# Value products of 512 columns with channels on the partitions, turned by VectorE and sixteen transfers, in a cross-attention kernel; set-up reordered

## The chip, the cores and the metric

The kernel runs on one core of a Trainium2 chip. The core has five engines that work side by side: TensorE (PE, with its weight loads shown apart as PEld), VectorE (DVE), ScalarE (ACT), GpSimd (POOL) and SyncE (SP), which here only issues transfers. SP and ACT issue transfers on hardware queues, POOL on a software queue; all are carried by the core's 16 DMA engines. The metric is the device time of one execution in microseconds (us); lower is better. The kernel before takes 1952.8 us, the median of three runs (1952.07 to 1952.91).

## The reference

The arrays `x` and `y` are (32, 256, 1024) in fp32: 32 batches of C = 256 channels and N = 1024 positions. The weights `w_qk`, `w_v`, `w_t` are 256 x 256.

```
x_q = einsum('oc,bcn->bno', w_qk, y)
x_k = einsum('oc,bcn->bon', w_qk, x)
x_v = einsum('oc,bcn->bon', w_v, x) + b_v
energy    = einsum('bnc,bcm->bnm', x_q, x_k)
attention = softmax(energy, axis=-1)
attention = attention / (1e-07 + attention.sum(axis=1, keepdims=True))
x_r = einsum('bcn,bnm->bcm', x_v, attention)
x_r = relu(einsum('oc,bcn->bon', w_t, x - x_r) + b_t)
return x + x_r
```

## The kernel before

**Weights are folded.** Set-up multiplies weights among themselves once: `gw` is w_qk with itself, so that the energy is y (gw x) and no query product is left; `vw` is w_v with w_t, so that what attention gathers is already through w_t; `tw` is w_t transposed. Biases are folded likewise (`xbias`, `ubias`, `nbias`).

**Three forms.** Every operand of a large product is kept in three forms, HIGH, LOW and REST (`FORMS = 3`), in fp32r: a rounded high part and two corrections with a scale of `UP = 4096` between them. A product of two operands is the sum over the three pairs of forms, all in one accumulation. With the 256 channels in two blocks of 128 (`KC = 2`), an output of 128 rows and 512 columns takes 3 x 2 = 6 matmuls, and one of 128 x 1024 takes 12. Such a set of twelve is the unit that the text calls a group.

**A batch** consists of these groups on TensorE, each named by a token:

- `k0`, `k1`: keys of the next batch, one block of 128 channels each (`keys`, `channels`); ScalarE and two passes of VectorE make the three forms `gf`.
- `v0`, `V1`: values, one half of the positions each (`values`). In the kernel before, x is the stationary operand: a matmul takes 128 positions as weights and `vw` as the 256 moving columns, so a half takes 4 x 3 x 2 = 24 matmuls of 256 columns and comes out with positions on the partitions, as attention needs it. `right` makes the three forms `uf[q]`: one pass of ScalarE and two of VectorE, straight from PSUM.
- `W0`, `W1`: the straight product of x with `tw` (`straight`), put by ScalarE into `xe`.
- `E0` to `E7`: energy for 128 query positions by 1024 keys (`energy`), then the softmax: a minimum over the row by VectorE, exponential with row sum on ScalarE, reciprocal, and the three forms `ef` by ScalarE, VectorE and GpSimd. VectorE adds the column sums up in `acc`.
- `A0` to `A7`: attention (`attention`), which adds `uf` times `ef` into banks 4 to 7 over the eight steps; the forms are taken in the order HIGH, REST, LOW (`ORDER`).
- `S` sums the columns (VectorE), `O` finishes the batch (`finish`): VectorE divides, GpSimd adds `xe`, ScalarE takes the ReLU, GpSimd adds x, SP stores. `X` loads the next x, `Y2` and `Y3` the next halves of y; GpSimd's queue makes two of the corrections by transfers that add.

**PSUM** has eight banks, used as four pairs. Pairs 2 and 3 hold the attention sums from A0 to the division; before A0 they are lent to the groups whose token ends in `^`. All others alternate between pairs 0 and 1. `uf` has one buffer for each half, `ef` four, `yf` two.

**What sets the order.** `Plan` takes each operation with an engine, a planned duration, a planned lag and the names that it reads and writes. TensorE works in the order of the tokens in `FIRST`, `STEADY`, `BEFORE` and `LAST` (first, middle, last but one and last batch) and `SET_UP`. On the other engines, transfers included, the planner runs through time and takes the operation that is due first; the order that comes out is fixed for each engine, and an engine does not go past an instruction that waits. The names and durations exist for the planner only: at run time an instruction waits for what the tiles that it really touches require. All calls go through one helper, so nearly every line of the profile reads L187, and the tile names tell the operations apart.

Lines touched: the token strings (124 to 138), `load_y` (276), `values` (368), `energy` (393), `finish` and its kin (485 to 586), the set-up's loads (602 to 612), `square`, `weights`, `turned`, `value_weights`, `biases` (626 to 747).

Of the kernel before, what the change touches and what calls it, by code (L numbers as in the profile page):

```python
# [16 lines left out]
class Plan:  # L17
# [124 lines left out]
def kernel(  # L142
# [28 lines left out]
    NE = 4  # L171

# [61 lines left out]

    few = const.tile([P, P], F32, name="few")
# [13 lines left out]
    xo = one.tile([P, N], F32, name="xo")  # L249
    xe = one.tile([P, KC, N], F32, name="xe")  # L250
# [8 lines left out]
    def pair(j):  # L259
        return banks[:, 2 * j : 2 * j + 2]  # L260
# [15 lines left out]
    def load_y(q, direct=False):  # L276
# [5 lines left out]
        by_sync(7.0, [], ["yr"], lambda: sync.dma_start(r, from_))  # L282
# [85 lines left out]
    def values(b, q, j_pair):  # L368
        p = pair(j_pair)
        for t in range(HT):  # L370
            for j in ORDER:

                def of(t=t, j=j):
                    for k in range(KC):
                        matmul(
                            p[:, t // 2, ts(t % 2, C)], xf[:, j, k, ts(q * HT + t, P)], vw[:, j, k],
                            t % 2 == 0 and j == ORDER[0] and k == 0, j == ORDER[-1] and k == KC - 1,
                        )

                on_pe(  # L380
                    KC, C, [f"vw{j}{k}" for k in range(KC)] + [f"xf{j}{k}{q}" for k in range(KC)], [in_pair(j_pair)[t // 2]], of
                )
        right(j_pair, [uf[q][:, j] for j in range(FORMS)], [[f"uf{q}{j}"] for j in range(FORMS)])
# [9 lines left out]
    def energy(b, n, jp):  # L393
        s, e = (b * MH + n // HT) % NY, n % NE
        both, at, f = pair(jp), in_pair(jp), ef[n % NE]
        for h in range(MH):
            for j in ORDER:

                def of(h=h, j=j):
                    for k in range(KC):  # L400
                        matmul(
                            both[:, h], yf[s][:, j, k, ts(n % HT, P)], gf[:, j, k, ts(h, MB)],
                            j == ORDER[0] and k == 0, j == ORDER[-1] and k == KC - 1,
                        )

                on_pe(KC, MB, [f"yf{s}{j}"] + [f"gf{j}{k}" for k in range(KC)], [at[h]], of)
# [51 lines left out]
    def sums(b):  # L458
# [11 lines left out]
        def small_ops():  # L470
# [9 lines left out]
            1.25, ["sc"], ["rc"],  # L480
# [3 lines left out]
    def finish(b):  # L484
        for c in range(KC):

            def of(c=c):
                p = flat(pair(2 + c))
                on_dve(
                    N, in_pair(2 + c) + ["rc", "bias"], [f"z{c}"],  # L490
# [7 lines left out]
                by_sync(6.0, [], ["xo"], lambda: sync.dma_start(xo, x[b, ts(c, P)]))  # L498
# [17 lines left out]
    def divided(c):  # L516

        for h in range(MH):

            def of(c=c, h=h):  # L520
                p = pair(2 + c)[:, h]
                on_dve(
                    MB, [in_pair(2 + c)[h], "rc", "bias"], [in_pair(2 + c)[h]],
                    lambda: dve.scalar_tensor_tensor(p, p, ubias[:, c], rc[:, ts(h, MB)], ALU.add, ALU.mult),
                )

            of()

    def beside(b, c):

        for h in range(MH):

            def of(h=h):
# [4 lines left out]
                    MB, [in_pair(2 + c)[h], "rc", "bias", f"stored{c}"], [piece],  # L538
# [63 lines left out]
    for k, (by, dma) in enumerate(((by_sync, sync), (by_act, act))):  # L602
        by(2.9, [], [f"wqk{k}"], lambda k=k, dma=dma: dma.dma_start(wqk[:, k], w_qk[ts(k, P)]), early=50.0)
    for h in range(MH):
        for k, (by, dma) in enumerate(((by_sync, sync), (by_act, act))):
            by(
                3.9 + h, [], [f"xr{k}{h}"],
# [3 lines left out]
    by_sync(6.0, [], ["wt"], lambda: sync.dma_start(wt, w_t.rearrange("(k p) c -> p k c", p=P)), early=25.0)  # L611
    by_act(6.0, [], ["wv"], lambda: act.dma_start(wv, w_v.rearrange("(k p) c -> p k c", p=P)), early=25.0)
# [13 lines left out]
    def square(bank, left, right, reads, writes):  # L626
        for i in range(KC):

            def of(i=i):
                for k in range(KC):  # L630
                    matmul(
                        banks[:, bank + i, :C], left[:, k, ts(i, P)], right[:, k], k == 0, k == KC - 1
# [4 lines left out]
    def weights(to, name, bank, by, d, d_name):  # L637

        for i in range(KC):

            def of(i=i):
# [9 lines left out]
                dve_in_sbuf(  # L651
                    C // 2, [f"{d_name}{i}", "xe0"], names[LOW],
                    lambda: dve.tensor_scalar(low, dd, UP, None, ALU.mult),
                )
# [51 lines left out]
    def turned():  # L706
# [21 lines left out]
    def value_weights():  # L728
        square(
            6, wv, wtT.rearrange("p (k c) -> p k c", k=KC), ["wv", "z0", "wtT", "acc0", "acc1"],  # L730
            [f"vwin{i}" for i in range(KC)],
        )
        weights(vw, "vw", 6, -UP, work[:, KC * C : 2 * KC * C], "vwd")

    def biases():
        by_sync(7.0, [], ["bv"], lambda: sync.dma_start(bv, b_v.rearrange("(o c) -> o c", o=1).to_broadcast([P, C])))
        by_sync(7.0, [], ["bt"], lambda: sync.dma_start(bt, b_t.rearrange("(k p o) -> p k o", p=P, o=1)))
# [11 lines left out]
    def set_up(token):  # L749
# [3 lines left out]
        elif token == "T":  # L753
            turned()
# [94 lines left out]
```

## Time and profile before

| | before |
|---|---|
| median of 3 runs | 1952.8 us |
| profiled execution | 1952.31 us |
| its span, first to last instruction | 1950.5 us |
| matmuls, busy (the same count of weight loads) | 9252, 1939.1 us |
| matmuls of the values, 128 x 256 | 1536, 196.5 us |
| VectorE, ScalarE, GpSimd busy | 1553.9, 1433.5, 1253.9 us |
| granted TensorE clock, mean | 0.998 |
| first matmul of V0 in the first batch | at 18.98 us |

The span leaves out 1.8 us of the profiled execution that lie around it. Busy time of TensorE is modelled for overlapping matmuls, so the pace is better read from the starts of consecutive groups. A row of instructions gives the total busy time, the mean of one, and after the bar how long the engine stood idle just before them and what ended that. A wait says who waited for whom, for how long in all, how often, and the longest.

### The profile page before, as it was taken

The page shows a single profiled execution, that of the slowest core. Times are in us where ns is not written, and L with a number is a line of the kernel's source. Part 1 is how long each engine was busy: PE and PEld are TensorE (multiplying, and loading weights), DVE is VectorE, ACT ScalarE, POOL GpSimd, SP SyncE. Part 2 cuts the span into 40 slices and gives each one's busy share as a digit, 9 for nine tenths or more (in the row PEclk, how much of TensorE's full clock was granted, in tenths as well). Part 3 has the DMA queues.
Part 4 walks back from the last instruction along what each step waited for, and adds up shares of the span by engine and source line. Part 5 has one row for each costly group of instructions (what it writes and reads, how often), then busy time and mean ns, then how long its engine had stood idle before and what let it go on. Part 6 is the DMA issues. An engine that isn't in the chain of part 4 may idle for free.

```text
span 1950.5 us, 25236 instructions
## 1 busy us (share of the span) xinstructions
PE 1939.1 (99%) x9252; PEld 1634.3 (84%) x9252; DVE 1553.9 (80%) x2177; ACT 1433.5 (73%) x1859; POOL 1253.9 (64%) x645
## 2 busy tenths in 40 slices
PE   8999999999999999999999999999999999999998
PEld 7888888888888888888888888888888888888887
DVE  7787887877887778878788877887877887778887
ACT  5778776787767877667877678776787767777675
POOL 4667665766656666566766577665766656666564
PEclk9999999999999999999999999999999999999999
DMA  4555545565455554455544555545564455554440
GB/s 128 129 119 141 123 108 115 119 148 123 112 105 130 140 127 118 109 125 127 137 119 104 126 119 141 125 110 111 121 149 121 116 104 128 139 130 118 110 98 33
DMA packets 81994, 234.28 MB, mean 120 GB/s; under 512 B 7504, under 2 KB 8656, under 8 KB 81872
## 3 DMA queue, kind: packets, MB, share of 16 engines
q0 software_dynamic: 35136, 98.58, 29.4%
q1 hardware_dynamic: 46032, 133.19, 21.1%
q8 instruction: 73, 1.20, 0.3%
q10 hardware_dynamic: 704, 0.92, 0.1%
q14 instruction: 49, 0.40, 0.1%
HBM read 133.56 MB, written 33.55 MB: 86 GB/s over the span
## 4 chain that ended last, share of the span: by engine, by line
PE 97%; DVE 2%; issue 0%; ACT 0%; DMA 0%; DVEq 0%
PE banks L187 97%; DVE xf L187 0%; DVE gf L187 0%; DVE ef L187 0%; DVE acc L187 0%; DVE z L187 0%; DVE vw L187 0%; DMA z<-in_L_xattn_w_qk_dram 0%; DVE small L187 0%; DVE parts L187 0%; DVE rc L187 0%; DVE xe L187 0%; DVE sc L187 0%; DVE gw L187 0%; ACT yf L187 0%
## 5 line engine op out<-in xcount | busy, mean ns | idle before, releaser
L187 POOL TENSOR_TENSOR ef<-ef 128x1024 fp32r<-128x1024 f32 x256 | 614.2, 2405 | 444.7 <-ACT ef L187 226.1
L187 PE MATMUL banks<-gf,yf 128*128 128x512 f32 x3072 | 728.4, 389 | 0.3 <-DVE gf L187 0.3
L187 PE MATMUL banks<-ef,uf 128*128 128x512 f32 x3072 | 722.5, 389 | 1.1 <-DVE acc L187 1.1
L187 PEld LDWEIGHTS banks<-ef,uf 128*128 128x128 f32 x3072 | 576.7, 188 | 121.4 <-DVE acc L187 1.1
L187 PEld LDWEIGHTS banks<-gf,yf 128*128 128x128 f32 x3072 | 574.5, 188 | 118.9 <-DVE gf L187 0.7
L187 DVE SCALAR_TENSOR_TENSOR ef<-banks,small,ef 128x512 fp32r<-128x512 f32 x512 | 378.7, 745 | 151.3 <-ACT ef L187 151.0
L187 DVE TENSOR_REDUCE small<-banks 128x1 f32<-128x1024 f32 x256 | 312.6, 1221 | 108.4 <-PE banks L187 106.3
L187 ACT ACTIVATE banks<-banks,small 128x1024 f32<-128x1024 f32 x256 | 276.9, 1082 | 134.4 <-DVE small L187 133.7
L187 ACT ACTIVATE ef<-banks,small 128x512 fp32r<-128x512 f32 x512 | 320.9, 690 | 40.5 <-DVE small L187 40.5
L187 DVE SCALAR_TENSOR_TENSOR acc<-banks,small,acc 128x512 f32<-128x512 f32 x448 | 329.7, 742 | 0.0
L187 POOL TENSOR_TENSOR z<-z,xe 128x1024 f32<-128x1024 f32 (+1 forms) x64 | 151.1, 2380 | 205.3 <-DVE z L187 205.3
L187 ACT ACTIVATE ef<-ef 128x1024 fp32r<-128x1024 f32 x256 | 268.9, 1068 | 12.5
L187 ACT ACTIVATE gf<-banks 128x1024 fp32r<-128x1024 f32 x64 | 65.3, 1021 | 190.2 <-PE banks L187 190.2
L187 PEld LDWEIGHTS banks<-vw,xf 128*128 128x128 f32 x1536 | 194.8, 194 | 8.1 <-ACT gf L187 3.3
L187 PE MATMUL banks<-vw,xf 128*128 128x256 f32 x1536 | 196.5, 285 | 2.9 <-DVE vw L187 2.9
L187 PE MATMUL banks<-xf,tw 128*128 128x512 f32 (+1 forms) x774 | 186.1, 389 | 0.8 <-DVE z L187 0.6
L187 PE MATMUL banks<-xf,gw 128*128 128x512 f32 x768 | 185.4, 390 | 0.3
L187 PEld LDWEIGHTS banks<-xf,gw 128*128 128x128 f32 x768 | 143.9, 188 | 30.9 <-DVE xf L187 0.6
L187 PEld LDWEIGHTS banks<-xf,tw 128*128 128x128 f32 x774 | 143.0, 189 | 29.5 <-DVE z L187 0.8
L187 POOL TENSOR_TENSOR z<-z,xo 128x1024 f32<-128x1024 f32 x62 | 157.7, 2544 | 9.0 <-DMA xo<-in_x_dram 9.0
L187 POOL TENSOR_TENSOR xf<-xr,xf 128x1024 fp32r<-128x1024 f32 (+1 forms) x64 | 151.2, 2388 | 5.7 <-DVE xf L187 4.6
L187 DVE RECIPROCAL small<-small 128x1 f32<-128x1 f32 x256 | 41.3, 161 | 114.8 <-ACT banks L187 113.5
(66 smaller groups left out, 1408.5 us busy)
## 6 DMA issues: line engine op xcount, KB each, us to landing
yr<-in_ctx_dram SPq DMA_DIRECT2D x64, 512.0 KB, 3.8
yf<-in_ctx_dram POOLq DMA_DIRECT2D x63, 512.0 KB, 6.7
yf<-yf POOLq DMA_DIRECT2D x63, 512.0 KB, 4.6
xo<-in_x_dram SPq DMA_DIRECT2D x62, 512.0 KB, 4.3
xr<-in_x_dram SPq DMA_DIRECT2D x62, 512.0 KB, 3.4
xf<-xf POOLq DMA_DIRECT2D x62, 512.0 KB, 6.9
out_dram<-z SPq DMA_DIRECT2D x62, 512.0 KB, 4.8
out_dram<-z SPq DMA_DIRECT2D x3, 256.0 KB, 2.1
```

What stands on the lines that cost most here:

```text
L187: self.last = getattr(self.engine, name)(*args, **kwargs)
```

## The change

**Values.** `values` now takes `vw` as the stationary operand and 512 positions as the moving columns: 12 matmuls of 512 columns, channels on the partitions. Attention still needs positions there, so the result is turned. VectorE transposes it from PSUM in blocks of 32 x 32 into a new tile `turned` (128 x 1024). Sixteen transfers on SP's queue, four for each of the four groups of 32 target partitions, put the blocks in their places in the buffer of `uf`'s REST form: each takes 32 partitions to 32 others, four runs of 64 numbers in each. The order of the columns of `vw` is permuted in `value_weights` so that the blocks fall right, and its scale is -1 in place of -4096. The forms then come from this fp32 copy in SBUF: ScalarE copies HIGH, GpSimd subtracts, ScalarE scales LOW, GpSimd subtracts again for REST. VectorE's two passes from PSUM go.

**Order.** The token strings are new. In the middle batches V1 stands first, E6 and E7 are neighbours, and `v0` moves from the end to behind A5. E0 takes its matmuls by form (HIGH, LOW, REST), both halves of the columns for each, and the others as before.

**Set-up.** The keys' matmuls of the first batch come in another order. The scaling that makes LOW of a weight goes from VectorE to ScalarE (`weights`). The LOW form of the first y is made by an adding transfer on GpSimd's queue, no longer by a subtraction on GpSimd (`Y_ON_POOL` is False). Planned durations of some loads are changed, and the loads of the first y, of the biases and of `xo` name more that the planner is to wait for.

The diff, cut to its core:

```diff
 SET_UP = (
-    "x1 x0 G fH00 T b fH10 fL10 fR00 fH11 fR11 Q fR10 fH01 fL00 y fL11 fL01 fR01"
+    "x0 G fR10 x1 fH11 T fH10 fH01 fH00 Q fL00 fL10 fL11 b y fR00 fR11 fL01 fR01"
 )
 FIRST = (
-    "V0^ W1 E0 E1^ V1 E2 W0^ E3 A0 A1 E4 E5 A2 A3 E6 A4 E7 X A5 A6 k1 Y2 S A7 Y3 k0 O v0"
+    "V0^ W1^ W0^ E0^ E1 E2 V1^ E3 A0 A1 E4 E5 A2 A3 E6 E7 A4 X A5 v0 Y2 k1 A6 A7 k0 Y3 S O"
 )
 STEADY = (
-    "W1^ E0^ E1 V1^ E2 W0^ E3 Y2 A0 A1 E4 E5 A2 A3 E6 X A4 E7 Y3 A5 S k1 A6 A7 k0 O v0"
+    "V1 E0^ E1 W0^ E2 W1^ E3 A0 A1 E4 E5 X A2 A3 E6 E7 A4 S A5 v0 Y2 A6 k1 k0 A7 O Y3"
 )
 BEFORE = (
-    "E0^ E1 W1^ E2 V1^ W0^ E3 A0 A1 E4 E5 A2 A3 X E6 E7 A4 S A5 A6 k1 A7 Y2 Y3 k0 O v0"
+    "W1 E0^ E1 V1^ E2 W0^ E3 A0 X A1 E4 A2 E5 Y2 E6 A3 A4 v0 E7 k0 Y3 A5 S A6 k1 A7 O"
 )
 LAST = (
-    "V1^ E0 E1^ E2 E3 A0 A1 E4 E5 A2 A3 R E6 E7 A4 A5 A6 W0 a0 S G0 a1 D1 F1"
+    "E0 E1^ E2 R V1^ E3 A0 A1 E4 E5 A2 A3 E6 E7 A4 A5 A6 W0 a0 S G0 a1 D1 F1"
 )
...
-        by_sync(7.0, [], ["yr"], lambda: sync.dma_start(r, from_))
+        by_sync(7.0 if b else 3.5, ["xr01", "xr11"] if b == 0 else [], ["yr"], lambda: sync.dma_start(r, from_))
...
-        if direct:
+        if direct and q == 0 and Y_ON_POOL:
             on_pool(
                 N, [name[LOW], name[REST]], [name[LOW]],
...
     def values(b, q, j_pair):
-        p = pair(j_pair)
-        for t in range(HT):
+
+        both, at, u = pair(j_pair), in_pair(j_pair), uf[q]
+        for i in range(KC):
             for j in ORDER:
 
-                def of(t=t, j=j):
+                def of(i=i, j=j):
                     for k in range(KC):
                         matmul(
-                            p[:, t // 2, ts(t % 2, C)], xf[:, j, k, ts(q * HT + t, P)], vw[:, j, k],
-                            t % 2 == 0 and j == ORDER[0] and k == 0, j == ORDER[-1] and k == KC - 1,
+                            both[:, i], vw[:, j, k, ts(i, P)], xf[:, j, k, ts(q, MB)],
+                            j == ORDER[0] and k == 0, j == ORDER[-1] and k == KC - 1,
                         )
...
-        right(j_pair, [uf[q][:, j] for j in range(FORMS)], [[f"uf{q}{j}"] for j in range(FORMS)])
+                on_pe(KC, MB, [f"vw{j}{k}" for k in range(KC)] + [f"xf{j}{k}{q}" for k in range(KC)], [at[i]], of)
+        on_dve(
+            N, at, ["turned"],
+            lambda: dve.transpose(
+                turned.rearrange("p (q i r) -> p i q r", i=KC, r=G32),
+                both.rearrange("p i (q r) -> p i q r", r=G32),
+            ),
+        )
+        raw = value(u[:, REST])
+        names = [f"uf{q}{j}" for j in range(FORMS)]
+        moves = [f"{names[REST]}{a}" for a in range(NG)]
+        for a in range(NG):
+
+            def of(a=a):
+                for g in range(NG):
+                    sync.dma_start(
+                        raw[ts(a, G32)].rearrange("p (t g r) -> p t g r", t=HT, g=NG)[:, :, g],
+                        turned[ts(g, G32)].rearrange("p (t a r) -> p t a r", t=HT, a=NG)[:, :, a],
+                    )
+
+            plan.add("sync", 1.6, 6.0, ["turned"], [moves[a]], of)
+        on_act(N, moves, [names[HIGH]], lambda: act.copy(u[:, HIGH], raw))
+        on_pool(
+            N, moves + [names[HIGH]], [names[LOW]],
+            lambda: pool.tensor_tensor(u[:, LOW], raw, value(u[:, HIGH]), ALU.subtract),
+        )
+        on_act(N, [names[LOW]], [names[LOW]], lambda: act.mul(u[:, LOW], value(u[:, LOW]), UP))
+        on_pool(
+            N, [names[LOW]], [names[REST]] + moves,
+            lambda: pool.tensor_tensor(u[:, REST], raw, value(u[:, LOW]), ALU.subtract),
+        )
...
-        for h in range(MH):
-            for j in ORDER:
...
+        steps = [(j, h) for h in range(MH) for j in ORDER]
+        if n == 0:
+            steps = [(j, h) for j in (HIGH, LOW, REST) for h in range(MH)]
...
-                by_sync(6.0, [], ["xo"], lambda: sync.dma_start(xo, x[b, ts(c, P)]))
+                by_sync(6.0, ["bias"], ["xo"], lambda: sync.dma_start(xo, x[b, ts(c, P)]))
...
-                dve_in_sbuf(
-                    C // 2, [f"{d_name}{i}", "xe0"], names[LOW],
-                    lambda: dve.tensor_scalar(low, dd, UP, None, ALU.mult),
-                )
+                on_act(C, [f"{d_name}{i}", "xe0"], names[LOW], lambda: act.mul(low, dd, UP))
...
-            [f"vwin{i}" for i in range(KC)],
-        )
-        weights(vw, "vw", 6, -UP, work[:, KC * C : 2 * KC * C], "vwd")
+            [f"vwin{i}" for i in range(KC)], lambda w: w.rearrange("p (q i r) -> p i q r", i=KC, r=G32),
+        )
+        weights(vw, "vw", 6, -1.0, work[:, KC * C : 2 * KC * C], "vwd")
```

More of the change, by code (lines that the diff above doesn't have):

```diff
@@ L171 @@
     NE = 4
+    Y_ON_POOL = False
     const = ctx.enter_context(tc.tile_pool(name="const", bufs=1))
@@ L249 @@
     xo = one.tile([P, N], F32, name="xo")
+    turned = one.tile([P, N], F32, name="turned")
     xe = one.tile([P, KC, N], F32, name="xe")
@@ L395, in energy, with of @@
         both, at, f = pair(jp), in_pair(jp), ef[n % NE]
-        for h in range(MH):
-            for j in ORDER:
[L399 to L403, printed above, removed]
-                        )
-                on_pe(KC, MB, [f"yf{s}{j}"] + [f"gf{j}{k}" for k in range(KC)], [at[h]], of)
+        steps = [(j, h) for h in range(MH) for j in ORDER]
+        if n == 0:
+            steps = [(j, h) for j in (HIGH, LOW, REST) for h in range(MH)]
+        begun = {h: [j for j, g in steps if g == h] for h in range(MH)}
+        for j, h in steps:
+            def of(j=j, h=h):
+                for k in range(KC):
+                    matmul(
+                        both[:, h], yf[s][:, j, k, ts(n % HT, P)], gf[:, j, k, ts(h, MB)],
+                        j == begun[h][0] and k == 0, j == begun[h][-1] and k == KC - 1,
+                    )
+            on_pe(KC, MB, [f"yf{s}{j}"] + [f"gf{j}{k}" for k in range(KC)], [at[h]], of)
         p = flat(both)
@@ L624, with square @@
     )
-    def square(bank, left, right, reads, writes):
+    def square(bank, left, right, reads, writes, blocks=lambda w: w):
         for i in range(KC):
@@ L631, in of @@
                     matmul(
-                        banks[:, bank + i, :C], left[:, k, ts(i, P)], right[:, k], k == 0, k == KC - 1
+                        banks[:, bank + i, :C], left[:, k, ts(i, P)], blocks(right[:, k]), k == 0, k == KC - 1
                     )
```

28 lines of the change are left out of this document (13 added, 15 removed).

## The prediction

> **What bounds the kernel now.** First the page: the span, the busy times, and the chain of work that ended last.
>
> ```profile
> span 1950.5 us, 25236 instructions
> PE 1939.1 (99%) x9252; PEld 1634.3 (84%) x9252; DVE 1553.9 (80%) x2177; ACT 1433.5 (73%) x1859; POOL 1253.9 (64%) x645
> ...
> PE 97%; DVE 2%; issue 0%; ACT 0%; DMA 0%; DVEq 0%
> ```
>
> TensorE carries 97% of the chain, so the kernel lasts as long as its matmuls plus its few stops. A busy PE need not be at its best pace, so I read the pace from the timeline of PE in a middle batch (start, duration, what).
>
> ```profile
> 935.90 3.04 PE L187 MATMUL banks<-vw,xf 128*128 128x256 f32 x24
> 938.78 2.91 PE L187 MATMUL banks<-gf,yf 128*128 128x512 f32 x12
> 941.52 2.88 PE L187 MATMUL banks<-xf,tw 128*128 128x512 f32 x12
> 944.24 2.88 PE L187 MATMUL banks<-gf,yf 128*128 128x512 f32 x12
> ...
> 976.88 5.60 PE L187 MATMUL banks<-ef,uf 128*128 128x512 f32 x24
> 982.32 2.88 PE L187 MATMUL banks<-xf,gw 128*128 128x512 f32 x12
> 985.04 3.04 PE L187 MATMUL banks<-vw,xf 128*128 128x256 f32 x24
> ```
>
> From start to start, twelve matmuls of 512 columns take 2.72 us (941.52 to 944.24, 982.32 to 985.04): 226.7 ns each. The values' 24 of 256 columns, which cover as many columns, take 2.88 us (935.90 to 938.78): 120 ns each. A batch has 20 groups of 2.72 and two of 2.88, 60.16 us, and every group here starts when the one before has run out its pace: no stop at all in the steady part. The stops are at both ends, as the waits of PE show.
>
> ```profile
> PE banks L187 <- DVE vw L187: 2.9, 1, 2.9
> PE banks L187 <- DMA z<-in_L_xattn_w_t_dram: 1.3, 1, 1.3
> PE banks L187 <- DVE acc L187: 1.1, 2, 0.8
> ```
>
> The busy times of that batch (its span; then PE, PEld, DVE, ACT, POOL; clock; DMA share; GB/s) say how much room the others have.
>
> ```profile
> 932.78:992.94 60.16, 60.16 (x290) 50.77 (x289) 47.98 (x67) 44.80 (x59) 39.27 (x21) 1.00 0.52 122
> ```
>
> **The change part by part.** *1. Wide products.* Each of the 64 value blocks becomes 12 matmuls of 512 columns with weights stationary and xf moving, which is the form of the straight products (xf,tw) and of the keys (xf,gw). Those take 2.72, so a block falls by 2.88 - 2.72 = 0.16 us, and 64 of them by **10.24 us**. All of it lies on PE, so all of it counts, as long as PE goes on without stops.
>
> The Trainium skill, "TensorE: Matmul & The Clock Gate", section "Back-to-back issue gap", gives a lone warm matmul N/2.4 + 2.5 ns, an estimate of 109.2 ns at 256 columns and 215.8 at 512, so that joining two saves only 2.5 ns and the whole change 1.9 us. The rows say 120 and 226.7, where joining saves 13.3 ns; I go by the rows.
>
> *2. What is done to the values.* These rows (all blocks; busy, mean ns of one) price what goes and what comes.
>
> ```profile
> L187 DVE SCALAR_TENSOR_TENSOR uf<-banks,uf 128x1024 fp32r<-128x1024 f32 x64 | 78.1, 1221 | 1.1
> L187 DVE SCALAR_TENSOR_TENSOR uf<-uf,banks 128x1024 fp32r<-128x1024 f32 x64 | 77.8, 1216 | 0.6 <-ACT uf L187 0.4
> L187 ACT ACTIVATE uf<-banks 128x1024 fp32r<-128x1024 f32 x64 | 65.8, 1028 | 77.5 <-PE banks L187 77.5
> L187 POOL TENSOR_TENSOR xf<-xr,xf 128x1024 fp32r<-128x1024 f32 x62 | 148.3, 2418 | 1.1 <-ACT xf L187 1.1
> L187 ACT ACTIVATE xf<-xf 128x1024 fp32r<-128x1024 f32 x62 | 66.6, 1076 | 0.0
> L187 ACT CAST xf<-xr 128x1024 fp32r<-128x1024 f32 x62 | 65.0, 1049 | 3.1
> L187 DVE STREAM_TRANSPOSE rc<-sc 128x1024 f32<-128x1024 f32 x32 | 39.8, 1245 | 1.1
> ```
>
> VectorE loses two passes (2.44 us) and gets one transpose. None here reads PSUM; the one row of a transpose is 1.245 us, the passes over PSUM 1.22, so I take 1.25, with 2.5 as the upper end if its scattered output halves the pace (then VectorE is back where it was). ScalarE: 1.03 goes, a copy of 1.05 and a scaling of 1.08 come. GpSimd gets two subtractions of 2.42 that it did not have. Per batch: VectorE 47.98 - 4.87 + 2.50 = 45.6 us, ScalarE 44.80 - 2.06 + 4.25 = 47.0, GpSimd 39.27 + 9.67 = 48.9, in 22 x 2.72 = 59.84 us. None becomes the bound by its sum; GpSimd goes to 82%.
>
> *3. The sixteen transfers.* Each moves 32 partitions x 4 runs of 64 numbers, 32 KB in runs of 256 B. No such transfer is in the trace. For the issue there are SP's rows (min/median/max ns), for landing the spread of the smallest and other transfers of z, and for the engines the queues (packets, MB, share of 16 engines).
>
> ```profile
> L187 SPq DMA_DIRECT2D xr<-in_x_dram x64: 327/339/467, 1.2 to 1795.7; - x64
> L187 SPq DMA_DIRECT2D z<-in_L_xattn_b_v_dram x1: 538/538/538, 4.2 to 4.2; - x1
> DMA to landing us min/median/max: 1.7/4.4/6.7
> ...
> q1 hardware_dynamic: 46032, 133.19, 21.1%
> q10 hardware_dynamic: 704, 0.92, 0.1%
> ```
>
> Issue: 16 x 0.34 to 0.54 = 5.4 to 8.6 us of SP. On the engines, 2048 packets a block. Upper end: a packet costs what SP's packets of 2.9 KB cost, 0.211 x 1950.5 x 16 / 46032 = 143 ns, so 2048 x 143 / 16 = 18.3 us of all engines, and beside the 0.52 that they are busy already 18.3 / 0.48 = 38 us. Lower end: by bytes, 49 ns a KB, 1.6 us. The nearest row is ScalarE's queue with packets of 1.3 KB: 0.1% x 1950.5 x 16 / 704 = 44 ns (rounding makes it 22 to 67). With 44 ns: 5.7 us, 12 beside the other traffic. I take 12 us from the first issue to the last landing, between 7 (5.4 and one landing of 1.7) and 38.
>
> On this price the Trainium skill points both ways: "DMA: Bandwidth & Descriptors", section "Specifications", says a transfer in runs under 512 B is done by read-modify-write, below line rate; its section "Why small descriptors are slow (HBM only)" exempts transfers within SBUF. No row here can decide.
>
> Who waits: the whole path to the value forms is 1.25 (transpose) + 12 + 1.05 + 2.42 + 1.08 + 2.42 + some 0.6 of handing over = 20.8 us, where it was 3.5. In the new order eleven groups lie between the end of v0 and the next batch's A0 (A6 k1 k0 A7 V1 E0 E1 W0 E2 W1 E3), 29.9 us, and A0 asks for the third form four matmuls later, 30.8. For V1 there are fourteen up to A4. So 10 us are to spare, and the transfers may last some 22. Behind the sixteen on SP stand the loads of x and y and the stores.
>
> ```profile
> SPq L187 <- POOL z L187: 996.7, 62, 36.5
> SPq L187 <- ACT yf L187: 479.5, 62, 13.2
> ```
>
> SP waits 1476 us of 1950 in these two rows alone; 64 x 8.6 = 550 us fit. The other danger is the reverse, a store that waits up to 36.5 us for GpSimd's z in front of the sixteen; by then z of the batch is long begun, so I count nothing, or, uncovered, the rival below.
>
> *4. Set-up and first batch.* VectorE is behind the stop of 2.9 us. Its row and PE's (timeline), ScalarE's pass over as many columns (groups), and the granted clock in one stretch (third number from the right):
>
> ```profile
> 15.44 3.06 DVE L187 TENSOR_SCALAR vw<-xe 128x256 fp32r<-128x256 f32 x2
> L187 ACT ACTIVATE vw<-banks 128x256 fp32r<-128x256 f32 x2 | 0.6, 368 | 0.0
> ...
> 18.98 5.46 PE L187 MATMUL banks<-vw,xf 128*128 128x256 f32 x24 [2.88 <-DVE vw L187]
> 24.24 3.28 PE L187 MATMUL banks<-xf,tw 128*128 128x512 f32 x12
> 27.36 5.60 PE L187 MATMUL banks<-gf,yf 128*128 128x512 f32 x24
> ...
> 19.00:21.00 2.00, 2.00 (x9) 2.00 (x10) 1.97 (x3) 0.00 (x0) 0.63 (x1) 0.50 0.00 0
> ```
>
> The four scalings of weights (3.06 us for the last two) go to ScalarE, at 0.37 each by its pass over 256 columns (the row above); the stop should shrink to some 0.3 us: -2.6. After it PE ran at a clock of 0.50, V0 taking 5.26 for 2.88 and W1 3.12 for 2.72: 2.78 more, which go with the stop. Against that, 8 us of VectorE (four passes for the keys, transpose, biases) now stand before E0, which starts three groups after V0, and the first A0 comes eight groups after V0's start, 21.8 us, and asks for the third form at 22.7: V0's own 2.7, up to 1.2 until VectorE is free, and 20.8 come to 24.7, so 1 or 2 us late, and a load of y ahead of the sixteen on SP would cost 3 or 4 more. I set 2.0 against it: **-3.4**, from -5.4 to 0. The low form of the first y by a transfer instead of a subtraction has 4 us of cover, and the loads' new reads are notes to the planner: the calls name no more tiles, so no wait is added. E0's new order moves no work: nothing.
>
> *5. The last batch.* The first A's stop there (the 1.1 us above) follows four E in a row; V1 now lies among them. I take **-1.0**, between -2 and +1.5.
>
> **The sum** against the profiled execution's own 1952.31 us (span 1950.5 and 1.8 around it): -10.2 - 3.4 - 1.0 = 1937.7. The median of the runs is 1952.8, 0.5 higher, so 1938.2, say **1938**; its own range is 1933 to 1943.
>
> **The rivals.** *The transfers come too late* (ends slower). Place: A0 of each batch. From 22 us on, each further us stops PE once a batch, 31 us in all; two over give 1938 + 62 = 2000. For it: the upper end of 38, and 52% of the engines busy. Against: the nearest packets are three times cheaper. Chance 0.11.
>
> *GpSimd late with the attention's low forms.* The row of the last ones:
>
> ```profile
> 973.71 2.39 POOL L187 TENSOR_TENSOR ef<-ef 128x1024 fp32r<-128x1024 f32 x1 [3.94 <-DVE ef L187]
> ```
>
> It ends at 976.1 for A6, which needs it eight matmuls after 976.88, at 978.7: 2.6 us over. One job of 2.4 in front is absorbed, two cost 2.2. If half a us a batch is lost, 15 to 16 in all: 1953, no change. For it: 82%, in order. Against: GpSimd waited 3.9 us for this input, so it is early. Chance 0.15.
>
> *Set-up and end bring nothing:* 1952.8 - 10.2 = 1942.6, up to 1945 with stops of the first A0. Chance 0.15.
>
> *The width does not pay:* the 0.16 us sits in the block's boundaries, not in the count of matmuls, and stays: 1952.8 - 4.4 = 1948.4. The rows of tw and gw, the very form, speak against it. By the page's gap of part 1 it would be 1946.5. Chance 0.05.
>
> **How the numbers follow.** The forecast has 0.54. About 0.2%, 3.9 us, is what runs of this kernel can tell from no change: 1948.9 to 1956.7. Faster: 0.54, of set-up 0.14, of GpSimd 0.03, of width 0.04: 0.75. Same: 0.08 of GpSimd and 0.01 each of set-up and width: 0.10. Slower: 0.11 and 0.04 of GpSimd: 0.15. The range goes from 1933 to 1955, which leaves the late transfers, GpSimd's worst part and 0.03 below outside.
>
> **What would show it.** Right: groups of xf,vw 128x512 every 2.72 us, batches 59.84 apart, V0 starting near 16.4 at a clock of 1.0, GpSimd near 81% and DMA near 0.7 busy. Wrong: PE waiting at A0 for GpSimd's uf (the transfers; their landing times then say how late), for ef (GpSimd's queue), or value groups still of 2.88. It would be most wrong if a stop came back in every batch: half a us there is more than all of set-up.

## The result, and the profile after

The change makes the kernel slower. After: **1966.93 us**, the median of four runs (1965.17 to 1968.28); before, on the same chip: 1952.43 (1951.91 to 1952.91). The ratio is 1.0076, 95% interval 1.0064 to 1.0088. The prediction was 1938, range 1933 to 1955.

The page of the kernel after: span and instructions, busy times, the main hardware queue (packets, MB, share of 16 engines), the chain of work that ended last.

```profile
span 1966.0 us, 25637 instructions
...
PE 1939.1 (99%) x8484; PEld 1589.7 (81%) x8484; DVE 1479.4 (75%) x2109; ACT 1448.1 (74%) x1927; POOL 1550.0 (79%) x773
...
q1 hardware_dynamic: 193488, 166.81, 29.9%
...
ACT 30%; PE 27%; SPq 15%; DVE 13%; issue 6%; DMA 6%; POOL 2%; DVEq 0%; ACTq 0%; POOLq 0%
```

No engine is near its limit but PE, and yet PE fell from 97% to 27% of the chain. ScalarE, VectorE and SP's queue carry 58% of it. The waits of the kernel after (us in all, times, longest) say what they wait for:

```profile
ACT uf L188 <- DMA uf<-turned: 196.4, 32, 8.1
...
DVE turned L188 <- DMA uf<-turned: 34.3, 15, 5.2
...
PE banks L188 <- DVE acc L188: 8.3, 5, 4.1
...
PE banks L188 <- ACT z L188: 3.6, 4, 1.2
PE banks L188 <- DVE vw L188: 2.9, 1, 2.9
```

PE waits for no `uf` to speak of. It is ScalarE that waits for the transfers, once a batch, 6 us each time. Two middle batches side by side, from V1's start to the next V1's start (columns as in the prediction's row):

```profile
937.07:996.91 59.84, 59.84 (x265) 49.55 (x264) 45.99 (x66) 45.19 (x60) 49.42 (x25) 1.00 0.64 147
996.91:1058.82 61.91, 60.66 (x265) 49.29 (x264) 45.53 (x66) 45.15 (x60) 47.69 (x23) 1.00 0.55 130
```

The first runs at exactly the predicted 59.84 us, 22 groups of 2.72. The second loses 2.07 us at the same clock. Its predecessors' v0 and what follows, from the timelines of the two batches (start, duration, engine, operation, idle before and its releaser):

```profile
926.77 1.24 DVE L188 STREAM_TRANSPOSE turned<-banks 128x1024 f32<-128x1024 f32 x1
...
941.10 1.05 ACT L188 CAST uf<-uf 128x1024 fp32r<-128x1024 f32 x1 [5.52 <-DMA uf<-turned]
...
943.97 1.09 ACT L188 ACTIVATE banks<-banks,small 128x1024 f32<-128x1024 f32 x1
...
986.23 1.25 DVE L188 STREAM_TRANSPOSE turned<-banks 128x1024 f32<-128x1024 f32 x1
987.40 1.21 DVE L188 TRANSPOSE_TENSOR_REDUCE parts<-acc 128x32 f32<-128x1024 f32 x1
987.51 13.14 SPq L188 DMA_DIRECT2D uf<-turned  x16
988.40 0.88 POOL L188 DMA_DIRECT2D yf<-yf  x1
...
1003.48 1.05 ACT L188 CAST uf<-uf 128x1024 fp32r<-128x1024 f32 x1 [8.06 <-DMA uf<-turned]
1003.63 1.25 DVE L188 STREAM_TRANSPOSE turned<-banks 128x1024 f32<-128x1024 f32 x1 [3.31 <-DMA uf<-turned]
...
1004.80 1.19 DVE L188 TENSOR_REDUCE small<-banks 128x1 f32<-128x1024 f32 x1
...
1006.02 1.09 ACT L188 ACTIVATE banks<-banks,small 128x1024 f32<-128x1024 f32 x1 [0.54 <-DVE small L188]
...
1014.55 2.97 PE L188 MATMUL banks<-gf,yf 128*128 128x512 f32 x12 [1.11 <-ACT z L188]
```

The CAST is the copy that makes HIGH, the first reader of what the sixteen transfers deliver. In the first batch it starts 13.1 us after the transpose ended (928.01 to 941.10), and E0's exponential 6.9 us after V1's start. In the second it starts 16.0 us after the transpose (987.48 to 1003.48); on VectorE V1's transpose waits as well, E0's minimum follows it, its exponential comes 9.1 us after V1's start, 2.2 later than in the other batch, and E3 stands for 1.11 us, which the profile puts down to ScalarE. E3 writes into the PSUM pair of E1, so it has to wait until E1's softmax, which comes behind E0's, has read that pair. The attention at A0, which the prediction watched, gets its forms in time.

This time from transpose to copy tells the loss batch by batch. Both rows are worked out from the timeline for some of the batches, the loss from key group to key group against 59.84 us:

```
v0 of batch (from 0)     2     3     4     5     6     7     8     9    10    11    12    16    17
transpose to copy, us  14.9  13.1  14.4  13.0  14.4  13.0  15.6  13.5  15.4  13.1  14.4  16.0  13.9
loss of that stretch   0.96  0.00  0.48  0.00  0.48  0.00  1.62  0.00  1.48  0.00  0.48  2.07  0.00
```

Up to 13.9 us nothing is lost, beyond that each us costs about one on the average. Single batches scatter (15.0 us cost 0.77 in batch 23, 15.3 us 2.10 in batch 24), but over v0 of the batches 2 to 29 the excess over 13.9 adds up to some 13.6 us and the losses to 14.2; v0 of batch 1, with 18.0, loses 6.0.

Where the 15.5 us of span went, after against before, from the starts of groups:

| stretch | us |
|---|---|
| start to V0 (18.98 to 19.77) | +0.8 |
| first batch | +2.4 |
| middle batches, stops | +20.0 |
| last batch | +2.6 |
| 64 groups of 2.72 in place of 2.88 | -10.2 |

### The profile page after: what moved, and what is told of

It reads as the page before. It is cut to its first block, busy times and chain, and to the rows that moved or that the text cites. A ratio compares the mean times of both kernels' runs of the same rounds, so it can differ in the third digit from the quotient of the medians.

```text
span 1966.0 us, 25637 instructions
## 1 busy us (share of the span) xinstructions
PE 1939.1 (99%) x8484; PEld 1589.7 (81%) x8484; DVE 1479.4 (75%) x2109; ACT 1448.1 (74%) x1927; POOL 1550.0 (79%) x773
## 3 DMA queue, kind: packets, MB, share of 16 engines
q8 instruction: 68, 1.11, 0.2%
## 4 chain that ended last, share of the span: by engine, by line
ACT 30%; PE 27%; SPq 15%; DVE 13%; issue 6%; DMA 6%; POOL 2%; DVEq 0%; ACTq 0%; POOLq 0%
PE banks L188 27%; SPq L188 15%; ACT ef L188 12%; ACT banks L188 5%; ACT xf L188 4%; DVE ef L188 4%; ACT yf L188 4%; DVE acc L188 3%; ACT uf L188 3%; DVE turned L188 2%; DMA uf<-turned 2%; DMA yr<-in_ctx_dram 2%; DVE small L188 2%; ACT xe L188 2%; POOL uf L188 1%
## 5 line engine op out<-in xcount | busy, mean ns | idle before, releaser
L188 POOL TENSOR_TENSOR ef<-ef 128x1024 fp32r<-128x1024 f32 x256 | 629.0, 2463 | 72.4 <-ACT ef L188 46.5
L188 POOL TENSOR_TENSOR uf<-uf 128x1024 fp32r<-128x1024 f32 x128 | 326.6, 2551 | 57.2 <-ACT uf L188 57.1
L188 ACT ACTIVATE ef<-banks,small 128x512 fp32r<-128x512 f32 x512 | 334.5, 715 | 1.1 <-DVE small L188 1.0
L188 ACT ACTIVATE banks<-banks,small 128x1024 f32<-128x1024 f32 x256 | 282.9, 1105 | 64.2 <-DVE small L188 64.2
L188 ACT ACTIVATE ef<-ef 128x1024 fp32r<-128x1024 f32 x256 | 275.9, 1099 | 0.2
L188 ACT CAST uf<-uf 128x1024 fp32r<-128x1024 f32 x64 | 68.5, 1070 | 196.4 <-DMA uf<-turned 196.4
L188 PE MATMUL banks<-xf,vw 128*128 128x512 f32 x768 | 184.6, 389 | 2.9 <-DVE vw L188 2.9
L188 PE MATMUL banks<-xf,gw 128*128 128x512 f32 x768 | 180.6, 390 | 2.8 <-DVE gw L188 2.8
L188 PEld LDWEIGHTS banks<-xf,vw 128*128 128x128 f32 x768 | 144.1, 188 | 33.2 <-DVE vw L188 3.3
```

What stands on the lines that cost most here:

```text
L188: self.last = getattr(self.engine, name)(*args, **kwargs)
```

## The experiments

### What the parts are worth

**Width alone**: the kernel before, its orders and set-up kept, only `values` with 512 columns; the forms are made as before, straight from PSUM.

```diff
-    p[:, t // 2, ts(t % 2, C)], xf[:, j, k, ts(q * HT + t, P)], vw[:, j, k],
+    both[:, i], vw[:, j, k, ts(i, P)], xf[:, j, k, ts(q, MB)],
...
```

> The kernel before with the value products alone made 512 columns wide (weights stationary); the three forms are made from PSUM as before and nothing is turned, so attention takes the values in the wrong layout. All theories: 64 x 0.16 us less, 1952.4 - 10.2 = 1942.2, between 1941 and 1944. If the width did not pay: 1952.

Measured: 1941.76 us beside 1951.98, ratio 0.9947 (0.9932 to 0.9961). That is -10.2 us, the term of the prediction to a tenth.

**No transfers**: the kernel after, in which the sixteen are not issued; the buffers that they would fill are set to zero once at the start.

```diff
              def of(a=a):
-                for g in range(NG):
-                    sync.dma_start(
...
+                pass
```

> The changed kernel without the sixteen transfers: the forms are made from whatever stands in the buffer (zeros at the start), so the values are left out of the result; all matmuls and all work of VectorE, ScalarE and GpSimd stay in the same order. Theory 1: no engine waits for transfers any more, 1948, between 1944 and 1953. Theory 2: GpSimd's load is untouched, 1963 or more. Theory 3: like theory 1; run e1 tells those two apart.

Measured: 1942.79, ratio 0.9954 (0.9940 to 0.9969), 1.2 us under my range. ScalarE's copy now comes 7.6 to 7.8 us after the transpose in the middle batches. The page shows GpSimd with as much work as after:

```profile
PE 1928.3 (99%) x8484; PEld 1592.8 (82%) x8484; DVE 1480.4 (76%) x2109; ACT 1450.7 (75%) x1927; POOL 1552.5 (80%) x775
```

So 1552.5 us of GpSimd and all the new passes of ScalarE cost nothing here. In the kernel after, too, PE's waits for GpSimd come to 0.5 us in all, those of its weight loads to 1.4. So GpSimd's lateness is ruled out as the cause. The run also shows that set-up, first and last batch bring nothing: with them the kernel is 1.0 us above the width alone, which is inside the intervals.

### What makes a transfer dear

**Longer runs**: sixteen transfers as before, but each 32 partitions x one run of 1 KB.

```diff
-                        raw[ts(a, G32)].rearrange("p (t g r) -> p t g r", t=HT, g=NG)[:, :, g],
-                        turned[ts(g, G32)].rearrange("p (t a r) -> p t a r", t=HT, a=NG)[:, :, a],
+                        raw[ts(a, G32), ts(g, C)],
+                        turned[ts(g, G32), ts(a, C)],
```

> The changed kernel with each of the sixteen transfers moving 32 partitions x one run of 1 KB in place of four runs of 256 B: the same 32 KB, a quarter of the runs; the values land in other columns than they should. Theory 1 with the issue priced by runs: an issue on SP falls from 0.60 us to about 0.35, the values land some 8 to 9 us after the first issue, inside the plan, and the time is near 1950. Theory 1 with the issue priced by instruction: 0.60 stays, and the time stays near 1966. Theory 3 (packets): fewer packets, near 1950 even if the issue stays at 0.60.

**Fewer transfers**: four of 128 partitions x 4 runs of 256 B, so the same bytes in the same runs.

```diff
-                for g in range(NG):
-                    sync.dma_start(
...
+                sync.dma_start(
+                    raw.rearrange("p (t g r) -> p t g r", t=HT, g=NG)[:, :, a],
+                    turned.rearrange("p (t a r) -> p t a r", t=HT, a=NG)[:, :, a],
+                )
```

> The changed kernel with four transfers of 128 partitions x 4 runs of 256 B in place of sixteen of 32 partitions: the same bytes in the same number of runs, but no block changes its partitions, so the values are in the wrong places. If SP's price is one per instruction (0.6 us): 4 x 0.65 + 2 to 3 us to land, some 5 us, and the time is that without transfers, 1943 to 1946. If the runs of 256 B or the engines' load were the price: as with sixteen, 1955 or more.

Measured: 1955.63 with longer runs (ratio 1.0021, 1.0011 to 1.0030), **1942.32** with four transfers (0.9949, 0.9934 to 0.9964), 0.7 us under my range. The rows of SP's queue, first of the kernel after, then with runs of 1 KB, then with four transfers (min/median/max ns):

```profile
L188 SPq DMA_DIRECT2D uf<-turned x1024: 585/599/2212, 24.1 to 1927.7; - x171
```

```profile
L188 SPq DMA_DIRECT2D uf<-turned x1024: 507/589/2953, 23.5 to 1914.7; - x171
```

```profile
L188 SPq DMA_DIRECT2D uf<-turned x256: 593/639/2496, 22.9 to 1895.1; - x128
```

One issue costs SP 0.6 us, whether it carries 32 KB or 128 KB, in runs of 256 B or 1 KB. Sixteen in a row, with 0.04 between, take 10.2 to 14.0 us, 11.5 in the median of the 64 blocks; four take 2.9 in the median. The time from transpose to copy, 13.0 to 16.0 us in the middle batches of the kernel after, falls to between 8.3 and 10.0. The stops in the middle are gone. The 24.6 us between 1942.3 and 1966.9 are therefore the price of the twelve further instructions on SP. The four also leave every block on its own partitions; that this matters is not shown, but the sixteen of 1 KB, which do cross partitions, were cheaper as well. The longer runs shorten the time from transpose to copy only to between 12.5 and 15.7, since the issues are still sixteen; but where about a us is lost for each us beyond 13.9, that is worth 11 us. The limit is the same in this run: 13.96 us cost 0.01, 14.29 cost 0.35, 15.65 cost 1.71. My expectation for that run had not seen this.

### What turns a late transfer into a stop

**A later place for the copy**: the planner is told a longer time for the transfers, 15.5 us in all in place of 12.4. Nothing but the order on the engines changes.

```diff
-            plan.add("sync", 1.6, 6.0, ["turned"], [moves[a]], of)
+            plan.add("sync", 3.0, 3.5, ["turned"], [moves[a]], of)
```

> The changed kernel with one planner's entry altered: each four of the sixteen transfers are planned as 3.0 us of SP and 3.5 us to landing (15.5 us in all) in place of 1.6 and 6.0 (12.4 us). TensorE's order and all the work stay; only the order on the other engines moves. Theory 1 (the transfers end later than planned, so ScalarE's copy of uf and VectorE's next transpose stand waiting in front of the softmax work): the stops of the middle batches, 17.3 us more than before the change, go, the losses at both ends stay: 1950, between 1946 and 1954. Theory 2 (GpSimd, 79% busy, is late with the low forms): the same work of GpSimd, so 1963 or more. Theory 3 (the 131 thousand short packets slow the other transfers): 1963 or more.

Measured: 1955.30, ratio 1.0016 (1.0007 to 1.0026), 1.3 us above my range; 11.6 us of the loss are back. The chain, and the copy's group (busy, mean ns, idle before), of this run:

```profile
PE 93%; DVE 2%; SPq 2%; ACT 1%; DMA 1%; issue 1%; DVEq 0%; ACTq 0%
```

```profile
L188 ACT CAST uf<-uf 128x1024 fp32r<-128x1024 f32 x64 | 66.7, 1043 | 4.1 <-DMA uf<-turned 3.7 <-issue 0.4
```

In the middle batches the copy now stands 16.5 to 17.2 us behind the transpose, behind E0's exponential, and does not wait: the transfers were not too late for the attention, the copy was too early in ScalarE's order. 196.4 us of waiting are 3.7. The middle batches still lose 9.8 us in all, 0.4 in most second ones and 2.1 in one; that one is taken up with the stops of "First batch in the old way" below. The first batch stays too. In it A0 comes eight groups after V0 and now does wait for the transfers:

```profile
47.88 6.42 PE L188 MATMUL banks<-ef,uf 128*128 128x512 f32 x20 [3.64 <-DMA uf<-turned]
```

**Copy or transpose?** In the kernel after two instructions wait for the transfers, ScalarE's copy and VectorE's transpose of V1, which needs `turned` free. Here V1 uses `rc`, idle at that time.

```diff
+        turn, t_name = (rc, RC) if q else (turned, ["turned"])
...
```

> The kernel after with one edit: V1's transpose writes into rc, which is idle from the division of the batch before to the next S, and no longer into turned, so that it never waits for v0's transfers. The planner's numbers stay. Theory A (ScalarE's copy, which stands in a fixed order and waits for the transfers, is what makes the middle stops): the 196 us of ScalarE's wait stay above 150, the stops in every second batch stay, 1962 to 1968 us. Theory B (VectorE's transpose waiting for the buffer turned makes them): VectorE's 34 us of wait go, the stops in the middle go with them, 1944 to 1950 us. If both share in it: 1951 to 1961.

Measured: 1967.98, ratio 1.0076 (1.0061 to 1.0091); no gain at all. The two groups of this run:

```profile
L188 ACT CAST uf<-uf 128x1024 fp32r<-128x1024 f32 x64 | 68.4, 1068 | 200.1 <-DMA uf<-turned 193.0 <-DMA uf<-rc 7.1
...
L188 DVE STREAM_TRANSPOSE turned<-banks 128x1024 f32<-128x1024 f32 x32 | 39.8, 1244 | 0.6 <-PE banks L188 0.5
```

VectorE's 34.3 us of waiting for the buffer are 6.4, in waits of 0.2 us at most, and the stops are as before. So the buffer is not needed for the stops, and of the two instructions that wait the copy on ScalarE is left as the cause. No run moves the copy alone: the run before this one moved other work of the engines with it.

**New orders, old values**: the kernel before with the five new token strings, no wide product and no transfer.

> The kernel before with the changed kernel's five token strings (set-up, first, middle, last but one, last); values, forms and loads as before, no transfers within SBUF. Theory 1 (the transfers cost the time, not the orders): within 4 us of before, 1948 to 1956, and the middle batches without stops. Rival (the orders themselves bring the stops of the middle batches): 17 us more, 1969.

Measured: 1964.73, ratio 1.0064 (1.0047 to 1.0081), outside what I expected. The middle has no stops (0.04 us a batch, as before), so the orders alone do not make them. The 12.4 us go at the ends: V0 at 20.71, 3.2 us in the first batch, 2.6 and 4.4 in the last two. With the new values and four transfers the same orders cost only 0.6 us beside the width alone, so it is the pair of new orders and old values that does not fit; why is open.

### Attempts at a version that keeps the gain

**First batch in the old way** (two kernels): its values 256 wide and straight from PSUM, the planner told 3.0 and 4.0, SET_UP of before; then also FIRST of before with v0 behind A5.

```diff
+        if b == 0:
...
+                                both[:, t // 2, ts(t % 2, C)], xf[:, j, k, ts(q * HT + t, P)],
+                                vw[:, j, k].rearrange("p (i q r) -> p q i r", i=KC, r=G32),
...
-            plan.add("sync", 1.6, 6.0, ["turned"], [moves[a]], of)
+            plan.add("sync", 3.0, 4.0, ["turned"], [moves[a]], of)
```

> A version meant to use the width: the changed kernel, with the transfers planned as 3.0 us for each four and 4.0 us to land, the set-up's token order of before, and the values of the first batch made in the old way (x stationary, 256 columns, forms from PSUM), so that no transfer stands before the first A0. Theory 1: the plan's correction gave 1955.3; the first batch's 3.6 us wait for the transfers and about 1 us of its other stops go: 1950, between 1946 and 1953. If the first batch's loss has another cause: 1955.

> As the version with the first batch's values in the old way, and with the first batch's token order of before (v0 moved behind A5). Theory 1: the first batch then loses what it lost before the change, 2.9 us in place of 7.7: 1949, between 1945 and 1952.

Measured: 1969.50 (ratio 1.0086, 1.0071 to 1.0101) and 1965.22 (1.0070, 1.0055 to 1.0085); both expectations missed. V0 comes at 20.31 and 20.70 and waits for `vw` as ever, and a new stop stands in every fourth batch, PE waiting for VectorE's `z`, 10.8 us and 11.6 us in all. `z` is the tile into which VectorE divides; SP stores it. One such stop of the first kernel, on SP, VectorE and PE:

```profile
444.39 13.70 SPq L188 DMA_DIRECT2D uf<-turned  x16
458.19 0.53 SPq L188 DMA_DIRECT2D out_dram<-z  x1
...
461.46 1.28 DVE L188 SCALAR_TENSOR_TENSOR z<-banks,ubias,rc 128x1024 f32<-128x1024 f32 x1 [1.69 <-DMA out_dram<-z]
...
462.80 3.02 PE L188 MATMUL banks<-xf,tw 128*128 128x512 f32 x12 [1.57 <-DVE z L188]
```

The division waits until the store of the batch before has landed. That store stands on SP behind the sixteen issues, and VectorE's waits for it come to 10.7 and 11.6 us, as much as PE's. So the chain of sixteen does harm at a second place: to what stands behind it on its own queue. With 3.0 and 3.5 planned the worst middle batch (2.1 us) is of this kind: sixteen issues of 13.69 us, VectorE's `z` 1.62 us late for the store, PE 1.51 us late for `z`.

**V1 later** (the planner told 3.2 and 4.5), and the same **with set-up and first batch of before**:

```diff
-    "V1 E0^ E1 W0^ E2 W1^ E3 A0 A1 E4 E5 X A2 A3 E6 E7 A4 S A5 v0 Y2 A6 k1 k0 A7 O Y3"
+    "W1 E0^ E1 V1^ E2 W0^ E3 A0 A1 E4 E5 X A2 A3 E6 E7 A4 S A5 v0 Y2 A6 k1 k0 A7 O Y3"
```

> The kernel after with the planner told 3.2 us of SP and 4.5 us of lag for each four of the sixteen transfers, and with STEADY as W1 E0^ E1 V1^ E2 W0^ E3 A0 ..., the rest of it as it was: V1 comes four groups later, so that its transpose no longer wants the buffer turned 11 us after v0's but some 19. My theory (the fixed order on ScalarE and VectorE puts the softmax behind work that waits for the transfers): the stops of the middle batches go, those that the planner's numbers alone left (0.39 us in alternate batches) too; the first batch keeps its loss of 7 to 8 us and the end some 7: 1946 to 1953 us. Rival (the sixteen transfers are too slow wherever they stand): 1960 or more. Rival (what is left in the middle comes from VectorE's z and not from turned): 1953 to 1957, as with the planner's numbers alone.

> The same with all of the set-up of before (order of the keys' matmuls, loads, the weights' LOW on VectorE, the first y's LOW subtracted by GpSimd) and with the first batch's values made in the old way, 256 columns wide and straight from PSUM; its order is FIRST of before with v0 behind A5. My theory (three parts: width -10.2, transfers nothing where they are given room, set-up and ends at the level of before): V0 at about 19.0, some 3 to 4 us lost in the first batch, none in the middle: 1942 to 1949 us, faster than the kernel before. Rival (the new set-up is worth its 3.4 us, and taking it away costs that): slower than the other kernel of this call by 2 us or more. Rival (transfers are too slow wherever they stand): 1955 or more.

Measured: 1956.78 (ratio 1.0026, 1.0016 to 1.0037) and 1962.06 (1.0052, 1.0037 to 1.0067). Both expectations missed. In both kernels the middle batches settle to 0.24 us of loss each, with v0's copy 17.4 to 17.9 us after the transpose. But the later place has a price of its own where the path to A0 is short. The first A0 of the one, and that of the third batch of the other:

```profile
49.97 6.79 PE L188 MATMUL banks<-ef,uf 128*128 128x512 f32 x20 [5.64 <-POOL uf L188]
```

```profile
192.07 6.25 PE L188 MATMUL banks<-ef,uf 128*128 128x512 f32 x20 [2.37 <-POOL uf L188]
```

Here GpSimd, whose subtractions follow the copy and queue behind others, is what A0 waits for. The second kernel lost 4.1 and 4.5 us in two of its first batches and had V0 only at 21.59, where the first had it at 19.23. It is 5.3 us slower than the first, as the rival that gives the new set-up a worth would have it; but the set-up of before has V0 at 18.98 in the kernel before and at 19.59 with the width alone, so this run does not settle what the set-up is worth.

**Buffer and planner together**: V1 in `rc`, and 3.0 and 3.5 as above.

> The same buffer for V1, and the planner told 3.0 us of SP and 3.5 us of lag for each four transfers, as in the first experiment (1955.3 us, whose middle batches lost 9.8 us, its first batch 7.7). My theory (what is left there comes from jobs that the planner placed, not from the buffer): the first batch still loses 7 to 8 us, since A0 comes eight groups after V0 whatever the buffer, and the middle some 6: 1951 to 1956 us. Rival (the buffer made the rest): 1944 to 1949 us, faster than the kernel before.

Measured: 1955.95 (ratio 1.0018, 1.0009 to 1.0028), as my theory had it and the same as without the buffer. The middle loses 7.0 us, and the first A0 again waits:

```profile
47.52 7.64 PE L188 MATMUL banks<-ef,uf 128*128 128x512 f32 x20 [3.63 <-POOL uf L188]
```

The three kernels at 1942 us do without the turning or do a part of it; of those that do all of it none came out below the kernel before.

## Why the prediction was wrong, point by point

**Width: right.** -10.24 predicted, -10.2 measured alone. The batches that aren't stopped take 59.84 us to the hundredth. The formula of the Trainium skill ("TensorE: Matmul & The Clock Gate", "Back-to-back issue gap"), by which it would have been an estimated 1.9 us, is given there for a lone matmul, and these products, each with a weight load, do not follow it: joining two saved 10.2 us / 768 = 13.3 ns.

**Transfers: the step that failed is "Who waits".** It took the deadline of the whole path, A0, and found 10 us to spare. That holds: with the copy at 16.5 to 17.2 us no A0 of a middle batch waits for it. What I left out are the path's own steps as members of fixed queues. ScalarE does not go past its copy, and behind the copy stand E0's and E1's exponentials, whose deadline is some 8 us nearer. The place of the copy was in the diff: four entries of 1.6 us and a lag of 6.0 let the planner count on it 12.4 us behind the transpose, ahead of E0's exponential; without the transfers ScalarE came to it after 7.6 to 7.8 us. The limit that was measured is 13.9 us, not 22. I wrote that "the transfers may last some 22" from A0 alone, though the section on the order of the work says that an engine does not go past an instruction that waits. SP's queue I judged by its idle time over the whole kernel (1476 us), and not by what stands behind the sixteen in each batch; where the orders were moved, the store there made stops of up to 2.5 us.

**The price of the transfers, mis-sized but not decisive.** I took 12 us from the first issue to the last landing, from packets. The copy came after 13.0 to 16.0. The size was near; its source was wrong. Of the two terms I made the packets the larger (5.7 us, 12 beside other traffic) and SP's issue the smaller (5.4 to 8.6). The issue is 0.60 us each, 10.2 to 14.0 us in a row, above my upper end, which came from a row of another kind of transfer. The packets of 256 B take 22 ns each, counted one by one in the trace, half of my 44: 2.9 us on the 16 engines for a block. Had I used 10.2 plus one landing of 1.7, I would have had the same 12, and with the limit that was measured a margin of 1.9 us: still no stop on paper, but a margin that two or three slow issues eat.

**Set-up: wrong, from -3.4 to about nothing.** Two of its three pieces did as said. The scalings left VectorE, and the clock stayed up. These are the rows of VectorE and PE after, with the clock in the same stretch (third number from the right):

```profile
15.53 1.77 DVE L188 TENSOR_TENSOR xe<-z 128x512 f32<-128x512 f32 x1
...
17.33 0.69 DVE L188 TENSOR_REDUCE wtb<-xe 128x2 f32<-128x512 f32 x1
...
18.39 0.75 DVE L188 SCALAR_TENSOR_TENSOR xe<-banks,vw 128x256 f32<-128x256 f32 x2
...
19.77 3.01 PE L188 MATMUL banks<-xf,vw 128*128 128x512 f32 x12 [2.90 <-DVE vw L188]
...
22.62 5.60 PE L188 MATMUL banks<-xf,tw 128*128 128x512 f32 x24
```

```profile
19.80:21.80 2.00, 2.00 (x9) 1.67 (x10) 0.99 (x2) 2.00 (x3) 1.30 (x1) 1.00 1.05 369
```

The biases (15.53 to 18.39) took the place on VectorE that the scalings (15.44 to 18.42) had. I had them after V0; they stand before `vw`. So the stop is 2.90 where it was 2.88, and V0 comes 0.8 later. The 0.8 belongs to this execution: in seven other kernels with the new set-up V0 starts at 18.55 to 19.23. In five of these the stop before V0 is under 0.4 us, as I had it, but the matmuls ahead of it end later, and V0 starts at most 0.2 us before the 18.98 of old. The clock gave 2.4 us back (V0 in 2.85 us where it took 5.26), and the first batch took them again: E3 waits 3.04 us for VectorE's `acc` and then takes 4.27 us (42.14 to 46.41) for its 2.72, at a granted clock of 0.64, and so all that was won is gone by the first A0. Part of that is the transfers again: ScalarE's copy waits 2.18 us for them there, and without them E3 waits 1.0 us and the first batch loses 3.0 us in place of 5.3 (2.9 before the change). Without the cost of the transfers (four of them, or none) the whole of set-up and both ends is worth +0.6 to +1.0 us over the width alone. My rival "set-up and end bring nothing", 1942.6, is what these two runs show.

**The last batch: wrong**, +2.6 for -1.0. The stop of 0.75 at the first A, for `acc`, is still there, and an E waits 1.07 us more for ScalarE's `ef`.

**Rivals.** "The transfers come too late" (0.11) had the right culprit; its place (A0), its threshold (22 us) and its price (31 us for each us over, from the mean) were wrong: the loss comes mostly in every second batch, because the time itself swings between 13 and 16 us. "GpSimd late" (0.15) is ruled out for the kernel after; it appears, with 2 to 6 us at single A0, only where the copy was moved late. Of what I named as signs, the groups of 2.72, the batches of 59.84 (those that are not stopped), the clock of 1.0 and GpSimd's share (79% for 81%) came; V0 near 16.4 did not, and neither did the sign of failure I named, PE at A0. The 0.64 and 0.55 of DMA share are under the 0.7, as the packets are cheaper.

## What to carry to other kernels

Where queues are fixed in order, an operation that depends on a transfer has two deadlines: that of its own result, and that of everything behind it on its engine. Read the second from the place in the queue, and compare it with the issue time of the whole chain of transfers, not only with the data they move. Ask the same of the queue that issues the chain: here a store behind it held a buffer back. If a layout change needs many small transfers, count the instructions on the issuing queue first: here twelve more of them cost 24.6 us with the same bytes in the same runs.

## What the runs showed of the hardware

An issue from SP within SBUF took 0.60 us in the median, from 32 KB to 128 KB and from runs of 256 B to 1 KB alike; the loads of x before took 0.34. In the kernel after 100 of the 1024 issues took more than 1.0 us, the longest 2.2. Of these 100, 94 began while an adding transfer of GpSimd's queue was on its way, of the other 924 only 350; in the second batch shown there are three, of 1.4 to 1.5 us. That the adding transfers are the reason was not tried. The chain of that batch's neighbour (start, us, what) shows the pace, one slow issue in it, and the last landing:

```profile
931.68 1.41 SPq L188
933.09 0.04 issue
933.13 0.62 SPq L188
933.76 0.04 issue
933.80 0.60 SPq L188
...
938.95 1.93 DMA uf<-turned
```

Packets of 256 B within SBUF took 22 ns of an engine each, those of 1 KB 60 ns (means over the trace of the kernel after and of the run with longer runs; each transfer adds 16 packets of 4 B at 9 ns). So short runs cost 1.5 times the engine time per byte, and with four transfers in the same short runs none of it cost the kernel time. The Trainium skill ("DMA: Bandwidth & Descriptors") lets transfers within SBUF off its rule against small descriptors in "Why small descriptors are slow (HBM only)"; the kernel's time agrees with four transfers (1942.3 us in runs of 256 B), while with sixteen the longer runs were worth 11 us, and by the engines' time the runs agree only in part.
